# When the sums of x and of the attended values are made: moving three kinds of GpSimd sums, and the block moves of one batch, between slots of a fused attention kernel

## The chip, the cores and the metric

The kernel runs on one NeuronCore of one Trainium2 chip. The metric is the device time of one execution in microseconds. The program's instructions go to TensorE (PE; its weight loads are listed apart as PEld), VectorE (DVE), ScalarE (ACT), GpSimd (POOL) and SyncE (SP). In this kernel SP only issues DMAs, one after the other, in program order. Each engine takes its own instructions in program order too; they wait for each other through semaphores.

## What is computed

A cross-attention block in float32, with 8 batches of 256 rows and 1024 columns, 32 heads of width 32, and 256 keys per batch:

```python
mu  = x.mean(-1);  var = x.var(-1)
xn  = (x - mu) * rsqrt(var + 1e-5) * gamma + beta
Q   = split_heads(xn @ Wq.T)                 # 32 heads of 32
K = V = split_heads(ctx)                     # ctx: 8 x 256 x 1024
p   = softmax(where(mask, Q K^T / sqrt(32), -inf))
out = x + merge_heads(p V) @ Wout.T
```

## The kernel before

**Slots.** A batch has 8 groups of 4 heads (`NQ = 8`), so there are `N = 64` groups, and the main loop runs over them: slot n is one pass of `for n in range(N)`. The b-th batch's own slots are 8b to 8b+7; "first slot" is 8b, "seventh slot" is 8b+6. In slot n the program issues, in this order: the scores of group n+1 on PE (`scores(n + 1)`, L479), some steps of the output product of the batch before (`project_steps(n, 0)`, L694), the attended values of group n-2 (`values(n - 2)`, L622), more output steps (`project_steps(n, 1)`), the queries of a later group (`make_q`, L340, or `query_product`, L440), the softmax of group n+1, then the side work of the slot, with `project_steps(n, 2)` in its middle.

**Softmax of one group.** For each of 4 heads and 2 row blocks, DVE adds the mask and takes the minimum (L515), ACT takes the exponential with its row sum (L519); per head, DVE takes the reciprocal (`rden`, L526), POOL multiplies by it twice (L528; the function is `normalize`), and DVE transposes 32x32 blocks into `pT` (L534; `blocks`). ACT copies half of `pT` aside into `pc` (L540), and SP moves quarters between partitions (L600 `pT<-pT`, L604 `pT<-pc`). PE uses `pT` of the group three slots later, in its `values`. There are 4 buffers of `e`, 4 PSUM banks of scores, 3 of `pT`.

**Two products made with 7 multiplications instead of 8.** For batches 3 to 7 (`SPLIT = 3`) the query product is Winograd's form of a 2x2 block product, one multiplication in each of 7 slots from `first = 8 (b - 1) + 2` on (`firsts`; `Q_PRODUCTS`). It needs four sums of quarters of the normalized x, all on POOL (`sum_x`, L430): S1 = A21 + A22 and S2 = S1 - A11 into the two halves of `sums_x`, S4 = A12 - S2 and S3 = A22 - S2. S1 is used in slot `first`, S2 in `first + 3`. The output product of batches 0 to 6 has the same form (`PRODUCTS`), with four sums of quarters of the attended values (`sum_at`, L675): S3 = A11 - A21 (written over A21), S2 = A22 - S3, S4 = A12 - S2, S1 = S2 + A11. The first half of a batch's attended values is complete in its slot 8b+5, the second half in slot 8b+9. For S3 only the first half is needed.

**The first steps of an output product.** For batches 0 to 5, in slot 8(b+1)+1 PE makes four steps of A11 (8 PE instructions), ACT copies that partial result out of PSUM (`keep_p1`, L702, placed in the softmax after the exponentials of three heads), and only then three steps of A12 go on in the same PSUM bank. This is the slot in which PE makes no queries (except slot 17, which makes one).

**x on its way in.** For a batch b from 2 on, x is loaded, its statistics are taken (`ln_stats`, L226 and L231 on DVE, a power on POOL, L234, behind the sums of the slot), ACT normalizes it, DVE transposes blocks (`blocks_x`), and 16 DMAs of 64 KB put the blocks in place (`move_x`, L327, tile names `xnT<-xe`). The moves of a slot are issued on SP behind the DMAs of that slot's softmax. Batches 3 to 7 have their moves in slots first-6, first-5 and first-4 (4, 6 and 6). Batch 2's moves are in slots 5 to 8, four in each; its queries are first made in slot 10.

**Weights.** POOL also folds gamma into Wq (`fold`, L361), makes four sums of quarters of Wout (`sum_wo`, L183) and four of Wq (`sum_wq`, L391), by hand-written lists of slots. `keep_wq` (L397, L400) sends finished sums to DRAM, `load_ring` (L407) brings them back.

The lists are consulted at the end of a slot, in this order: moves, `keep_wq`, the mask's bias, `project_steps(n, 2)`, `sum_at`, `sum_x`, `add_p1`, the power of the statistics, and the sums of weights.

## Time and profile before

| | |
|---|---|
| time before, median of 3 runs | 592.53 us (591.06 to 595.61) |
| profiled execution, its own time | 590.59 us |
| its span | 588.8 us |
| granted TensorE clock, mean over the span | 0.994 |
| PE busy | 572.1 us, 97% |
| DVE / ACT / POOL busy | 453.9 / 412.1 / 396.7 us |
| DMA queue q1 | 117.74 MB, 67.8% of 16 engines' span |
| POOL idle ahead of S1 of x (L430), 4 times | 22.6 us |

The span is the time from the program's first to its last instruction in the profiled execution; the 1.8 us between 588.8 and 590.59 lie around it. A row of the groups gives the engine, the line, output and inputs, how often, then busy time and mean duration, and after the bar the idle time of the engine just ahead of it with what ended it. A busy PE is not PE at its peak: the ends of matmuls are modelled, and a matmul under a halved clock counts as busy for longer.

A slot can be found in the trace by the 16 matmuls of L479 with which it begins; the times of slots in this document are the starts of those groups.

### The profile page before, as it was taken

The numbers are of one execution on the slowest core, as the hardware profiler recorded it, in microseconds if no ns is written. First come the engines' busy times: TensorE is split into PE (matmuls) and PEld (weight loads), VectorE is DVE, ScalarE is ACT, GpSimd is POOL, SyncE is SP. The second block draws the span as 40 slices with busy tenths as digits, with TensorE's granted clock in tenths as the row PEclk, the third lists the DMA queues.
The fourth block names the chain that finished last, engine by engine and source line by source line (L and its number), as shares of the span: only waits on it lengthen the run. The fifth ranks groups of instructions, "written<-read, shape, count | busy, mean of one in ns | idle before, by whom it ended". The sixth has DMA issues, their size and how long they took to land.

```text
span 588.8 us, 20015 instructions
## 1 busy us (share of the span) xinstructions
PE 572.1 (97%) x7176; PEld 395.1 (67%) x7176; DVE 453.9 (77%) x1686; ACT 412.1 (70%) x1424; POOL 396.7 (67%) x663
## 2 busy tenths in 40 slices
PE   8999998999999999899999999799998999999997
PEld 8778884676676776577766776467774777754544
DVE  6898898787778887888888888678876778779801
ACT  4688877776578775796777877578775766769810
POOL 1787999789788985766576762857628466458720
PEclk9999999999999999999999999999998999999999
DMA  8675798755886777876878666776657764547661
GB/s 291 240 217 174 218 259 230 248 154 171 248 247 175 236 207 220 226 221 175 241 210 245 190 186 187 241 211 201 169 140 224 221 203 141 143 121 224 177 184 71
DMA packets 48051, 119.02 MB, mean 202 GB/s; under 512 B 9168, under 2 KB 9936, under 8 KB 47952
## 3 DMA queue, kind: packets, MB, share of 16 engines
q1 hardware_dynamic: 47664, 117.74, 67.8%
q8 instruction: 57, 0.93, 0.8%
q14 instruction: 42, 0.34, 0.2%
q10 hardware_dynamic: 288, 0.01, 0.0%
HBM read 66.33 MB, written 11.53 MB: 132 GB/s over the span
## 4 chain that ended last, share of the span: by engine, by line
PE 71%; DVE 7%; DMA 6%; POOL 6%; issue 4%; ACT 3%; SPq 2%; POOLq 0%; DVEq 0%; ACTq 0%
PE po_S L694 16%; PE pq L340 9%; PE pq_A L440 9%; PE sc L479 9%; PE pv L622 8%; PE po_A L694 7%; PE pq_S L440 6%; POOL e L528 4%; DMA pT<-pT 3%; PE po L744 3%; DVE pT L534 3%; ACT e L519 2%; DVE e L515 2%; DMA x<-in_x_dram 1%; PE po_last L744 1%
## 5 line engine op out<-in xcount | busy, mean ns | idle before, releaser
L528 POOL TENSOR_SCALAR e<-e,rden 128x256 f32<-128x256 f32 x512 | 236.4, 482 | 124.5 <-DVE rden L526 123.1
L519 ACT ACTIVATE e<-e,mn 128x256 f32<-128x256 f32 x512 | 254.0, 501 | 54.6 <-DVE mn L515 54.6
L534 DVE STREAM_TRANSPOSE pT<-e 128x512 f32<-128x512 f32 x256 | 180.8, 706 | 60.1 <-POOL e L528 51.1
L515 DVE CUSTOM_DVE_ANT_0 e<-sc,mb 128x256 f32<-128x256 f32 x512 | 186.0, 416 | 32.6 <-PE sc L479 32.3
L540 ACT COPY pc<-pT 128x512 f32<-128x512 f32 x128 | 79.0, 617 | 78.9 <-DVE pT L534 39.8
L519 ACT ACTIVATION_READ_ACCUMULATOR e<-e,mn 128x1 f32 x512 | 97.8, 191 | 0.0
L340 PE MATMUL pq<-xnT,wq 128*128 128x256 f32 (+1 forms) x368 | 84.2, 383 | 2.4 <-DMA xnT<-xe 2.4
L340 PEld LDWEIGHTS pq<-xnT,wq 128*128 128x128 f32 x368 | 68.6, 190 | 17.1 <-issue 3.8
L479 PEld LDWEIGHTS sc<-k,qa 32*128 32x128 f32 x1024 | 46.4, 185 | 43.6 <-issue 25.5
L622 PE MATMUL pv<-pT,v 64*32 64x128 f32 x4096 | 74.5, 274 | 0.0
L694 PE MATMUL po_S<-wo,at 128*128 128x512 f32 x152 | 74.3, 606 | 0.0
L622 PEld LDWEIGHTS pv<-pT,v 64*32 64x32 f32 x4096 | 57.2, 105 | 25.3 <-issue 11.9
L479 PE MATMUL sc<-k,qa 32*128 32x256 f32 x1024 | 74.0, 402 | 0.1
L694 PE MATMUL po_A<-wo,at 128*128 128x512 f32 x128 | 63.9, 635 | 9.6 <-ACT p L702 8.1
L694 PE MATMUL po_S<-wo,s 128*128 128x512 f32 x104 | 50.1, 605 | 0.0
L694 PEld LDWEIGHTS po_A<-wo,at 128*128 128x128 f32 x128 | 23.2, 195 | 36.0 <-issue 22.8
L515 DVE DVE_READ_ACCUMULATOR2_ANT mn<- 128x1 f32 x512 | 42.6, 83 | 0.0
L526 DVE RECIPROCAL rden<-den 128x2 f32<-128x2 f32 x256 | 37.7, 147 | 5.7 <-ACT e L519 4.5
L440 PEld LDWEIGHTS pq_A<-xnT,wq 128*128 128x128 f32 x320 | 37.3, 192 | 4.8 <-issue 4.1
L694 PEld LDWEIGHTS po_S<-wo,at 128*128 128x128 f32 x152 | 25.8, 190 | 19.8 <-issue 19.1
L440 PE MATMUL pq_A<-xnT,wq 128*128 128x128 f32 x320 | 37.3, 275 | 0.0
L635 ACT COPY at<-pv 128x128 f32<-128x128 f32 x128 | 26.2, 254 | 10.3 <-PE pv L622 10.3
(89 smaller groups left out, 595.3 us busy)
## 6 DMA issues: line engine op xcount, KB each, us to landing
v<-in_kv_dram SPq DMA_DIRECT2D x32, 512.0 KB, 5.2
pT<-pT SPq DMA_DIRECT2D x128, 128.0 KB, 3.3
pT<-pc SPq DMA_DIRECT2D x128, 128.0 KB, 4.4
ring<-kept_T SPq DMA_DIRECT2D x18, 512.0 KB
k<-in_kv_dram SPq DMA_DIRECT2D x32, 256.0 KB, 3.9
x<-in_x_dram SPq DMA_DIRECT2D x14, 512.0 KB
r<-in_x_dram SPq DMA_DIRECT2D x28, 256.0 KB, 5.1
out_dram<-r SPq DMA_DIRECT2D x28, 256.0 KB, 3.0
```

Source lines behind the costliest of these rows:

```text
L340: nc.tensor.matmul(pqs[n], wq[:, o, c, :], xnTs[b](c), start=(c == 0), stop=(c == NC - 1),)
L440: nc.tensor.matmul(pqs[b][:, o, :], w[:, c], x_[:, c], start=begins and o + c == 0, stop=c == NK - 1, skip_group_check=True,)
L479: nc.tensor.matmul(scs[n][j][:, s, :], qa[r, n % NQ, ts(s, P)], ks[n - n % 2][r, n % 2, :], start=True, stop=True,)
L515: nc.vector.tensor_tensor_reduce(out=e[:, s, :], in0=pss[j][:, s, :], in1=mbs[n // NQ], scale=1.0, scalar=NO_SCORE, op0=ALU.add, op1=ALU.m ...
L519: nc.scalar.activation(e[:, s, :], e[:, s, :], AF.Exp, bias=mn[:, s : s + 1], scale=-1.0, accum_out=den[:, s : s + 1],)
L526: nc.vector.reciprocal(rden, dens[j])
L528: nc.gpsimd.tensor_scalar(es[j][:, s, :], es[j][:, s, :], rden[:, s : s + 1], 1.0, ALU.mult, ALU.mult,)
L534: nc.vector.transpose(pT[:, :, :, j, :, :].rearrange("p a i s k -> p (a i) s k"), es[j].rearrange("p s (b t) -> p b s t", t=K),)
L540: nc.scalar.copy(pc[:, :, ts(j, 2)], pT[:, 1, :, ts(j, 2)])
L622: nc.tensor.matmul(pvs[n][r][j * HD : (j + 1) * HD], vs[n - n % 2][ts(r, 2 * K), i, ds(n % 2 * P + j * HD, HD)], pT[ts(r, 2 * K), :, i, j, ...
L635: nc.scalar.copy(ats[b, k][:, c, :, ts(r, 2), :], pv.rearrange("p a s k -> p s a k"))
L694: nc.tensor.matmul(po, operand(b, name)[:, c], wo[:, which, c], start=begins and c == 0, stop=c == NK - 1, skip_group_check=not begins,)
```

## The change

Four edits, all of them in when something is issued; no instruction is added or taken away.

1. **Sums of x.** S1 and S2 of batch b are both made in slot first-2 = 8(b-1), S1 ahead of S2. Before, S1 stood in first-3 for batches 4 to 7 and in first-2 for batch 3, S2 in first-2 for batches 4 to 7 and in first-1 for batch 3. S4 (first-1) and S3 (first+1) stay.
2. **S3 of the attended values.** Batch 0 keeps slot 8. Batch 1 has it in slot 15 instead of 16, batches 2 to 6 in their own seventh slot 8b+6 instead of 8b+8.
3. **Batch 2's moves of x.** Slots 5, 6 and 7 with 4, 6 and 6 moves, instead of four slots with 4 each.
4. **Sums of Wq.** T3's second block goes from slot 15 to 16, its third from 16 to 17; the DMA that keeps its first half goes from slot 16 to 17.

```diff
         elif b == 2:
             when = dict(
                 loads=(0, 1), stats=(2, 3), norms=(3, 3), trans=(4, 5),
-                moves=tuple(5 + i // 4 for i in range(16)),
+                moves=tuple(5 + (i + 2) // 6 for i in range(16)),
             )
...
-        (9, "T1", 0), (14, "T1", 1, 2), (15, "T1", 3), (15, "T3", 0, 1), (16, "T3", 2),
-        (18, "T3", 3), (19, "T2", 0), (20, "T2", 1, 2, 3), (21, "T4", 0, 1), (22, "T4", 2, 3),
+        (9, "T1", 0), (14, "T1", 1, 2), (15, "T1", 3), (15, "T3", 0), (16, "T3", 1),
+        (17, "T3", 2), (18, "T3", 3), (19, "T2", 0), (20, "T2", 1, 2, 3), (21, "T4", 0, 1), (22, "T4", 2, 3),
     ):
         sums[n] += [partial(sum_wq, which, o) for o in chunks]

+    S3_SLOTS = [(b, NQ * b + {0: NQ, 1: NQ - 1}.get(b, NQ - 2)) for b in range(B - 1)]
...
-        (9, "B11", 0), (10, "B11", 1), (15, "T1", 0), (16, "T1", 1), (16, "T3", 0), (19, "T3", 1),
+        (9, "B11", 0), (10, "B11", 1), (15, "T1", 0), (16, "T1", 1), (17, "T3", 0), (19, "T3", 1),
     ):
         away[n].append(partial(keep_wq, name, half))
...
         project_steps(n, 2)
+        for one, slot in S3_SLOTS:
+            if n == slot:
+                sum_at(one, "S3")
         if b >= 0:
-            for name in {0: ("S3",), 2: ("S4",), 3 if b == B - 2 else 5: ("S1",)}.get(i, ()):
+            for name in {2: ("S4",), 3 if b == B - 2 else 5: ("S1",)}.get(i, ()):
                 sum_at(b, name)
             if i == 0 and b == B - 2:
                 sum_at(b, "S2", slice(0, NK - 1))
-        for slot, name in ((n + 3, "S1"), (n + 2, "S2"), (n + 1, "S4"), (n - 1, "S3")):
-            if slot in firsts and firsts[slot] > SPLIT:
+        for slot, name in ((n + 2, "S1"), (n + 2, "S2"), (n + 1, "S4"), (n - 1, "S3")):
+            if slot in firsts:
                 sum_x(firsts[slot], name)
-        for slot, name in ((n + 2, "S1"), (n + 1, "S2"), (n + 1, "S4"), (n - 1, "S3")):
-            if firsts.get(slot) == SPLIT:
-                sum_x(SPLIT, name)
```

## The prediction

> **What bounds the kernel now.** I read the page first, then the waits, then the slots. The page's busy times and its chain:

> ```profile
> PE 572.1 (97%) x7176; PEld 395.1 (67%) x7176; DVE 453.9 (77%) x1686; ACT 412.1 (70%) x1424; POOL 396.7 (67%) x663
> PE 71%; DVE 7%; DMA 6%; POOL 6%; issue 4%; ACT 3%; SPq 2%; POOLq 0%; DVEq 0%; ACTq 0%
> ```

> PE is the bound: 97% busy, 71% of the chain. An edit that moves only POOL and SP work pays only where PE stands still. The waits show what POOL and PE lose:

> ```profile
> POOL sx L430 <- DMA xnT<-xe: 18.4, 3, 6.7
> POOL sx L430 <- DMA out_dram<-r: 4.2, 1, 4.2
> PE po_A L694 <- ACT p L702: 8.1, 4, 2.3
> PE pq L340 <- DMA xnT<-xe: 2.4, 1, 2.4
> ```

> POOL waits 22.6 us in four places ahead of S1 of x, for block moves that have not landed (the fourth is put down to `out_dram`, which SP issues right behind the moves). PE waits 8.1 us for the copy of P1, and 2.4 us once for moves. The timeline of slots 47 to 49 ties the first to the third:

> ```profile
> 434.47 3.75 SPq L327 DMA_DIRECT2D xnT<-xe  x6
> 441.39 1.26 POOL L430 TENSOR_TENSOR sx<-xnT 128x512 f32<-128x512 f32 x1 [6.16 <-DMA xnT<-xe]
> 442.64 1.84 POOL L528 TENSOR_SCALAR e<-e,rden 128x256 f32<-128x256 f32 x4
> 445.61 0.62 ACT L540 COPY pc<-pT 128x512 f32<-128x512 f32 x1 [3.56 <-DVE rden L526]
> 451.45 0.56 ACT L702 COPY p<-po_A 128x512 f32<-128x512 f32 x1
> 452.06 4.54 PE L694 MATMUL po_A<-wo,at 128*128 128x512 f32 x6 [2.33 <-ACT p L702]
> ```

> S1 (slot 47) sits 6.16 us in front of the normalizes of slot 48, so these start at 442.64. ACT's `pc` copy, behind them, comes 3.56 us late, the exponentials of slot 49 after it, then the copy of P1, and PE waits for that. The windows of slots 9, 10, 25, 33, 41 and 49 give the price (length, then PE busy, PEld, DVE, ACT, POOL, granted clock):

> ```profile
> 88.30:97.09 8.79, 8.70 (x95) 4.10 (x95) 6.74 (x29) 7.33 (x24) 8.59 (x14) 1.00 0.92 259
> 97.09:108.13 11.04, 8.63 (x104) 5.63 (x103) 8.73 (x31) 7.03 (x23) 9.87 (x16) 1.00 0.75 232
> 230.16:241.29 11.13, 8.70 (x95) 4.10 (x94) 9.50 (x32) 6.49 (x22) 9.38 (x17) 1.00 0.68 189
> 300.85:310.61 9.76, 8.63 (x95) 4.10 (x94) 8.13 (x29) 6.49 (x22) 8.59 (x15) 1.00 0.70 208
> 370.27:383.75 13.48, 10.00 (x96) 4.38 (x95) 10.90 (x34) 7.11 (x23) 11.74 (x21) 0.90 0.73 229
> 443.64:456.53 12.89, 10.40 (x96) 4.54 (x95) 9.71 (x32) 7.11 (x23) 11.15 (x18) 0.87 0.72 227
> ```

> Slots 9, 25, 33, 41 and 49 hold the same PE work. Slot 9 has no S1 ahead of it and takes 8.79; the others take 9.76 to 13.48, longer the longer POOL waited (4.2, 5.6, 6.2, 6.7 us give 9.76, 11.13, 12.89, 13.48).

> **S1 and S2 of x in slot first-2.** S1 now comes one slot later. Does it still wait? POOL was released, so the moves had landed, at 227.34, 296.65, 368.50 and 441.39 at the latest. In an undisturbed slot the normalizes end 7.75 us after its scores start (slot 39: scores 354.05, last normalize 361.80). Slots 24, 32, 40 and 48 start at 222.51, 293.20, 362.56 and 435.99, so S1 would be reached at 230.3, 301.0, 370.3 and 443.7: after the landing by 2.9, 4.3, 1.8 and 2.3 us. No wait. The cover of 1.8 to 4.3 us is what a later landing could use up before PE pays.

> POOL then makes S1 and S2 in a row: 1.27 + 1.28 = 2.55 us, to 232.8 in slot 24. The first reciprocal of slot 25 comes 3.5 us after its scores (354.05 to 357.54 in slot 39), at 233.7: 0.9 us later. Before, that slot held S3 of the attended values and S2 of x, as many. What is late next is the power of the statistics in slots 23, 31 and 39, until now behind S1: its input is ready at 224.1 (DVE 223.95 + 0.15), the normalizes it stands before start at 226.0. Nothing.

> With the wait gone, ACT starts the exponentials of slot 25 some 1.7 us (slot 48: 435.99 to 437.68) to 2.44 us (slot 9: 88.30 to 90.74) after the scores; 3.5 us later (448.49 to 452.01) the copy of P1 ends, at 5.2 to 5.96 us. PE reaches A12 at 1.08 + 3.63 + 1.09 = 5.8. So PE waits 0 to 0.16, as in slot 9. I take 8.79 for each: 2.34 + 0.97 + 4.69 + 4.10 = 12.1, and 0.34 from slot 42, whose start still ran at half clock (8.85 against 8.51 in its like): **12.4 us**. The ends: 13.1 with no wait at all (8.63), 11.3 if the four still wait some 0.4 us.

> [...] The gaps here are 2.3 us, yet the clock falls to 0.90 and 0.87 in just the two slots with the longest stalls, and their PE busy time rises from 8.70 to 10.00 and 10.40. [...] By the rows they belong to the stalls (in slot 41 a second one of 1.16 us precedes) and go: 12.4. All slots with short stalls show 1.00; I take the rows.

> **S3 of the attended values, two slots earlier.** Its input is complete one slot before, so no wait. It adds 1.28 us to POOL in slots 22, 30, 38, 46 and 54. In slot 46 and its likes POOL idles 2.7 us on the reciprocal: hidden. Slot 22 is full: T4's last two sums stand behind S3 and end at 217.4 instead of 216.1, the third at 216.1. PE's A22 product of slot 23 starts at 217.13 and comes to that third block 1.8 us later, at 218.9: 2.8 us of cover, so 0; 1.28 us if it is gone. In slot 15 S3 falls into 2.42 us in which POOL waits for the statistics (150.3 to 152.7): free.

> [...]

> **Batch 2's moves in three slots.** Before, the last four go out in slot 8, at 98.26 to 101.3, and PE's queries of slot 10 start at 102.79 instead of about 100.2. Now slot 7's six go out from 90.80 to about 94.6; with the median 3.2 us to landing they are there at 98: 2 us of cover. Slot 10 falls from 11.04 to its PE busy 8.63: **2.4 us**. On SP slots 6 and 7 carry two issues more, 2 x 0.62 = 1.2 us, and slot 8 four fewer (3.05 us). Behind slot 7's moves stands `pT<-pT` at 93.98; the values that it feeds start at 109.2. Hidden. What is late next is POOL, which idles only 0.3 us a slot up to there: in slot 11 its work before ends at 109.1, and its first normalize, 111.70, would now be due at 109.3. Just enough; if POOL cannot follow, the gain is 0 to 1.7.

> **T3 and its DMA.** One POOL sum passes from slot 15 to 16 and one from 16 to 17, as S3 comes into slot 15 and S2 of x into 16: 3 sums of 512 columns in each of the three slots, as before. The DMA (0.41 us of SP) goes from 167.43 to about 173.7; T2's first sum, which overwrites what it reads, starts at 189.89. Nothing.

> **Sum.** 12.4 + 2.4 = 14.8 us. Against the profiled execution's own 590.59 (span 588.8 and 1.8 around it) that is 575.8; this execution is 1.9 us under the median of 592.53, which gives 577.7 for a median. I say 577.5.

> **Rivals.** *ACT stays the bound of slot first-1.* The copy of P1 comes behind six exponentials in any case. If every such slot stops at the mildest now seen, 9.76, the gain is 1.4 + 3.7 + 3.1 + 0.3 + 2.4 = 10.9: 581.6. For it: slots 33 and 9 differ by only 1 us. Against it: in slot 33 ACT's `pc` copy is late by a POOL wait too (1.79 us). *The waits of POOL are not PE's.* Then only slot 10 gains: 590.1. Against it: the order of the four lengths follows the four waits. *The wait moves along with S1 (slower).* SP issues the moves behind `pT` copies that POOL's normalizes pace. If with these earlier the last move came as late against S1 as now, POOL would wait 22.6 us one slot nearer to the P1 copy, with 0.9 us of slack each instead of about 3: 19 us on PE instead of 9.1, and four half-clock stretches instead of two, +3.4, less the 2.4 of slot 10: 592.5 + 10.9 = 603.4. It decides from landings over 2.7 to 5.2 us later (1.8 to 4.3 plus 0.9). Against it: these moves belong to slot first-4, and nothing ahead of them changes.

> **Chances.** Forecast 0.72, ACT bound 0.18, only slot 10 0.06, slower 0.04. A measurement of this kernel can tell about 1% from no change, 5.9 us; the first two pass it. So faster 0.90, same 0.06, slower 0.04. The range goes from 573.0 (13.1 + 2.4 off 590.59, and some 2 us for the run) to 584.0 (past the first rival, with half of slot 10's gain lost).

> **What would show it.** In the changed profile the row `sx<-xnT` has no idle time ahead of it and slots 25, 33, 41 and 49 take 8.6 to 9.0 us at a clock of 1.00; PE's wait for P1 falls from 8.1 to under 1; `pq L340 <- DMA xnT<-xe` is gone and slot 10 takes about 8.6. Wrong if a wait ahead of `sx<-xnT` of over 2 us stays, if slots 25 to 49 stay over 9.7 without it, or if slots 11 to 16 grow by what slot 10 loses.

## The result, and the profile after

The changed kernel takes 578.68 us (median of 4 runs, 577.78 to 578.80), the kernel before beside it 593.16 us (591.06 to 595.61): 0.9751 of the time, 95% interval 0.9711 to 0.9791, which is 14.5 us with an interval of some 12.4 to 17.1. In a second set of runs the same changed kernel came to 0.9729 (0.9701 to 0.9756) of the kernel before. Runs over 1.5% above the fastest of their set are left out of all ratios and means here. The profiled execution took 578.70 us, its span 576.9 us; that is 11.9 us under the profiled execution of before, which was one of its faster runs.

The page of the changed kernel: busy time of the engines, then the chain by engine.

```profile
PE 568.4 (99%) x7176; PEld 393.6 (68%) x7176; DVE 454.1 (79%) x1686; ACT 411.7 (71%) x1424; POOL 397.6 (69%) x663
PE 80%; POOL 7%; DVE 4%; DMA 4%; issue 2%; ACT 1%; SPq 1%; DVEq 0%; POOLq 0%; ACTq 0%
```

The instructions are the same in number. PE went from 97% to 99% busy, from 71% to 80% of the chain, and its busy time itself fell by 3.7 us: nearly all of that is time at half clock which is gone (1.4, 1.8 and 0.3 us in slots 41, 49 and 42). The longest waits of POOL, then those of PE (engine, line, what ended the wait, us in total, times, longest):

```profile
POOL e L528 <- DVE rden L526: 125.8, 92, 4.7
POOL rstd L234 <- DVE ve L231: 24.0, 8, 6.9
POOL r L720 <- ACT ends L712: 0.7, 1, 0.7
```

```profile
PE pq L285 <- DMA wq<-in_wq_dram: 1.4, 1, 1.4
PE busy L120 <- POOL ring masks.py:199: 1.3, 1, 1.3
PE po_A L694 <- issue: 0.8, 1, 0.8
PE po_S L694 <- DVE r L736: 0.7, 2, 0.4
PE po_A L694 <- DMA wo<-in_woT_dram: 0.6, 1, 0.6
PE po_A L694 <- ACT qa L349: 0.4, 1, 0.4
```

No row of `sx` is left: 22.6 us of POOL's waiting ahead of S1 are gone. PE's 8.1 us for the copy of P1 and its 2.4 us for the moves are gone too. POOL now waits longer for the statistics (24.0 against 17.2 us), ahead of which S1 used to stand, and nobody waits for that. What is new are short waits of PE for Wout and for `qa` (for `r` it waited before too, 1.3 us), and 1.4 us for a load of Wq ahead of slot 0. The windows of slots 9, 10, 25, 33, 41 and 49 (length, then busy time of PE, PEld, DVE, ACT and POOL, granted clock, DMA share, GB/s):

```profile
89.11:99.21 10.10, 8.97 (x96) 4.02 (x95) 7.85 (x31) 7.33 (x24) 9.79 (x16) 1.00 0.92 254
99.21:108.19 8.98, 8.62 (x103) 5.62 (x102) 5.37 (x25) 4.33 (x16) 4.75 (x7) 1.00 0.80 250
231.02:239.58 8.56, 8.56 (x95) 4.10 (x94) 6.47 (x26) 5.97 (x21) 6.51 (x11) 1.00 0.90 272
299.85:308.42 8.57, 8.57 (x96) 4.11 (x95) 6.49 (x26) 5.97 (x21) 6.54 (x12) 1.00 0.82 263
367.98:376.55 8.57, 8.57 (x96) 4.11 (x95) 6.49 (x26) 5.97 (x21) 6.54 (x12) 1.00 0.94 320
436.10:444.66 8.56, 8.56 (x95) 4.10 (x94) 6.31 (x25) 5.97 (x21) 6.17 (x11) 1.00 1.02 329
```

Slots 25, 33, 41 and 49 take 8.56 to 8.57 us, all of it PE busy, at a clock of 1.00. Slot 10 lost 2.05 us, but slot 9 took on 1.31.

Between the two profiled executions the time by slot moved so: slots 25, 33, 41 and 49 by -2.57, -1.20, -4.91 and -4.33, slot 42 by -0.34, slot 10 by -2.05, slot 9 by +1.31, slots 11, 15 and 26 by +0.28, +0.50 and +0.72; the stretch ahead of slot 0 was 0.78 longer. All other slots are within 0.07 us of before.

### The profile page after: what moved, and what is told of

Read it like the earlier page. It is cut to its first block, busy times and chain, and to the rows that moved or that the text cites. A ratio compares the mean times of both kernels' runs of the same rounds, so it can differ in the third digit from the quotient of the medians.

```text
span 576.9 us, 20009 instructions
## 1 busy us (share of the span) xinstructions
PE 568.4 (99%) x7176; PEld 393.6 (68%) x7176; DVE 454.1 (79%) x1686; ACT 411.7 (71%) x1424; POOL 397.6 (69%) x663
## 4 chain that ended last, share of the span: by engine, by line
PE 80%; POOL 7%; DVE 4%; DMA 4%; issue 2%; ACT 1%; SPq 1%; DVEq 0%; POOLq 0%; ACTq 0%
PE po_S L694 18%; PE pq_A L440 16%; PE pv L622 10%; PE sc L479 10%; PE po_A L694 10%; PE pq_S L440 6%; PE pq L340 6%; POOL e L528 5%; PE po L744 3%; DVE e L515 2%; DMA wo<-in_woT_dram 2%; PE po_last L744 1%; DMA wq<-in_wq_dram 1%; ACT e L519 1%; DVE pT L534 1%
## 5 line engine op out<-in xcount | busy, mean ns | idle before, releaser
L528 POOL TENSOR_SCALAR e<-e,rden 128x256 f32<-128x256 f32 x512 | 237.0, 483 | 127.3 <-DVE rden L526 125.8
L540 ACT COPY pc<-pT 128x512 f32<-128x512 f32 x128 | 79.0, 617 | 71.7 <-DVE pT L534 43.0
L340 PE MATMUL pq<-xnT,wq 128*128 128x256 f32 (+1 forms) x368 | 84.1, 383 | 0.0
L340 PEld LDWEIGHTS pq<-xnT,wq 128*128 128x128 f32 x368 | 68.7, 190 | 14.3 <-issue 3.9
L694 PE MATMUL po_S<-wo,at 128*128 128x512 f32 x152 | 74.5, 607 | 0.3 <-DVE r L736 0.3
L694 PE MATMUL po_A<-wo,at 128*128 128x512 f32 x128 | 61.0, 609 | 1.9 <-issue 0.8
L694 PE MATMUL po_S<-wo,s 128*128 128x512 f32 x104 | 50.2, 606 | 0.4 <-DVE r L736 0.4
L526 DVE RECIPROCAL rden<-den 128x2 f32<-128x2 f32 x256 | 37.5, 147 | 6.2 <-ACT e L519 4.9
L694 PEld LDWEIGHTS po_A<-wo,at 128*128 128x128 f32 x128 | 22.5, 189 | 26.9 <-issue 21.7
L694 PEld LDWEIGHTS po_S<-wo,at 128*128 128x128 f32 x152 | 25.6, 190 | 20.8 <-issue 19.3
```

The costliest lines, as they stand in the source:

```text
L340: nc.tensor.matmul(pqs[n], wq[:, o, c, :], xnTs[b](c), start=(c == 0), stop=(c == NC - 1),)
L526: nc.vector.reciprocal(rden, dens[j])
L528: nc.gpsimd.tensor_scalar(es[j][:, s, :], es[j][:, s, :], rden[:, s : s + 1], 1.0, ALU.mult, ALU.mult,)
L540: nc.scalar.copy(pc[:, :, ts(j, 2)], pT[:, 1, :, ts(j, 2)])
L694: nc.tensor.matmul(po, operand(b, name)[:, c], wo[:, which, c], start=begins and c == 0, stop=c == NK - 1, skip_group_check=not begins,)
```

## The experiments

Two theories to begin with. **W**: the wait ahead of S1 is the loss of slots 25 to 49, by the path S1, normalizes, ACT, copy of P1, PE. Its rival **R**: what counts is how much work POOL has in a row, and the room that S3 leaves. For slot 10, the prediction's 2.4 us stood against **Q**, formed from the profile after: the earlier moves hand the time on through SP's queue to slots 9, 11 and 15.

### One edit at a time

**The sums of x alone.**

```diff
-        for slot, name in ((n + 3, "S1"), (n + 2, "S2"), (n + 1, "S4"), (n - 1, "S3")):
-            if slot in firsts and firsts[slot] > SPLIT:
+        for slot, name in ((n + 2, "S1"), (n + 2, "S2"), (n + 1, "S4"), (n - 1, "S3")):
+            if slot in firsts:
                 sum_x(firsts[slot], name)
-        ...
```

> The kernel before with the edit of the sums of x alone (S1 and S2 in slot first-2); S3 of the attended values, batch 2's moves and T3 stay as before. Theory W (POOL's wait for landed moves ahead of S1, which passes through the normalizes and ACT to the copy of P1, is the whole gain): some 12 us below before, about 581, with no idle time ahead of the row sx<-xnT and slots 25, 33, 41 and 49 at 8.6 to 9.2 us. Rival R (the room that the moved S3 leaves on POOL is needed): slot first-2 now carries three sums, 3.8 us, 0.4 us past the first reciprocal of slot first-1, so slots 25 to 49 stay at 9.5 or more and at least a third of the gain is missing, 585 or more.

579.33 us, 0.9791 (0.9749 to 0.9833): 12.4 us of 592, with an interval of 9.9 to 14.9. Slots 25, 33, 41 and 49 take 8.56 to 8.57. POOL's busy time there is about one sum higher than in the changed kernel (7.80 and 7.73 in slots 25 and 33, against 6.51 and 6.54):

```profile
230.87:239.44 8.57, 8.57 (x96) 4.11 (x95) 6.54 (x26) 5.97 (x21) 7.80 (x13) 1.00 0.93 318
299.56:308.12 8.56, 8.56 (x95) 4.10 (x94) 6.48 (x26) 5.97 (x21) 7.73 (x13) 1.00 0.72 197
```

R falls: a third sum in slot first-2 costs nothing. This edit alone is nearly the whole of the change.

**S3 of the attended values alone** (the list `S3_SLOTS` and its loop, put into the kernel before).

> The kernel before with S3 of the attended values in its new slots alone. Theory W: the wait ahead of S1 stays (about 22 us of POOL in four places), so within 1 us of before; POOL's sums in slots 24, 32, 40 and 48 are one fewer, which may take up to 1.3 us off each of slots 25, 33, 41 and 49, if those are late by POOL's work and not only by its wait: then up to 5 us below before. Rival R (room on POOL is what counts): 6 us or more below before.

592.54 us, 0.998 (0.9943 to 1.0017): no difference. POOL still waited 22.3 us ahead of S1, and slots 25 to 49 took 9.63 to 12.71.

**Batch 2's moves alone.**

```diff
-                moves=tuple(5 + i // 4 for i in range(16)),
+                moves=tuple(5 + (i + 2) // 6 for i in range(16)),
```

> The kernel before with the edit of batch 2's moves alone (4, 6 and 6 in slots 5 to 7). The prediction's step: slot 10 falls from 11.04 to 8.6 and nothing else grows, 2.4 us below before. Theory Q (SP's queue hands it on: the two further moves of slot 6 hold back the loads of x and of Wout behind them, those of slot 7 the load of the residual, and POOL, which has no time to spare up to slot 16, sets the pace there): slot 10 falls by about 2 us, slots 9, 11 and 15 grow by as much together, start of slot 0 to start of slot 16 within 0.5 us of before, time within 1 us of before.

588.20 us, 0.9947 (0.9910 to 0.9984): 3.1 us, with an interval of 0.9 to 5.3. In its profiled execution slot 10 fell to 9.50, but slots 9 and 15 grew to 10.07 and 8.94, and PE waited for Wout and for `r`, as the changed kernel's did (here in slots 9 and 10):

```profile
97.63 1.13 PE L694 MATMUL po_A<-wo,at 128*128 128x512 f32 x2 [0.98 <-DMA wo<-in_woT_dram]
106.31 1.96 PE L694 MATMUL po_S<-wo,s 128*128 128x512 f32 x4 [0.88 <-DVE r L736]
```

In this execution slot 0 to slot 16 took 129.4 us, against 128.8 in the kernel before: no gain there, as Q says. That its time still lay 4.6 us below the profiled execution of before came from slots 25, 33, 41 and 49: 41.8 us together against 47.3, with the wait ahead of S1 still in place. These stalls differ from one execution to the next (44.1 with S3 alone), so the timed 3.1 us cannot be put down to the length of slot 10.

**The changed kernel without that edit.**

> The changed kernel with batch 2's moves back in slots 5 to 8. The prediction's step: 2.4 us above the changed kernel, 581. Theory Q: within 0.7 us of the changed kernel (578.0 to 579.4), slot 10 back at 11.0, slots 9, 11 and 15 back at 8.8, 9.25 and 8.45.

579.22 us, 0.9804 (0.9751 to 0.9857). Slots 9, 10, 11 and 15 were back at 8.84, 11.07, 9.25 and 8.39. Against 0.9751 and 0.9729 of the changed kernel it is 3 to 4.5 us more, with intervals that overlap: it favours the prediction's 2.4 without proving it. The single runs say where it comes from. The changed kernel's ten, over both sets, lay between 575.7 and 578.8 us, all at a mean granted clock of 0.999 or 1.00. Of the six here, three at a clock of 1.00 took 576.9 to 578.5, as long as the changed kernel; the other three, at 0.997, took 580.0 to 583.2. So in these few runs the old moves cost nothing where the clock held; the loss came with the lower clock. One stretch of 3.41 us at half clock is 0.003 of the mean, and the only pause of PE over 2 us in the profiled execution is the one of slot 10 (2.37 us).

### Is it the wait, or S1's place?

**S1 stays in slot first-3, the moves land one slot earlier.** In the kernel before:

```diff
-                moves=tuple(first - 6 + (i + 2) // 6 for i in range(16)),
+                moves=tuple(first - 6 + i // 8 for i in range(16)),
```

> The kernel before, S1 left in slot first-3, but the moves of batches 3 to 7 in two slots of eight (first-6 and first-5) instead of three, so that they land one slot ahead of S1. Theory W (the wait for the moves is the loss, wherever S1 stands): no or little idle time ahead of sx<-xnT, slots 25, 33, 41 and 49 at 8.6 to 9.0, clock 1.00, some 12 us below before, about 581. Rival (POOL's order of work is the loss: S1 behind slot first-3 holds back the normalizes also without a wait, by its own 1.27 us): half of the gain or less, 587 or more.

580.33 us, 0.9833 (0.9779 to 0.9888). The waits of POOL in this kernel:

```profile
POOL rstd L234 <- DVE ve L231: 19.9, 8, 7.2
POOL sx L430 <- DMA xnT<-xe: 1.3, 2, 0.7
```

1.3 us ahead of S1 where there were 22.6, and slots 25 to 49 at 8.56 to 8.57. W is shown from the other side: with S1 where it was and only the landing made earlier, the stalls are gone. The time came out 2.5 us higher than with the sums moved, within both intervals; in this execution slot 10, with its moves as before, took 12.4 us, and its pause of 2.10 us was followed by half clock. The one timed run at a clock of 1.00 took 577.2 us, the other five, at 0.997 or less, 579.7 to 583.5.

**S1 and S2 one more slot later**, in first-1, from the changed kernel:

```diff
-        for slot, name in ((n + 2, "S1"), (n + 2, "S2"), (n + 1, "S4"), (n - 1, "S3")):
+        for slot, name in ((n + 1, "S1"), (n + 1, "S2"), (n + 1, "S4"), (n - 1, "S3")):
```

> The changed kernel with S1 and S2 of x yet one slot later, in first-1 with S4 behind them: three sums of x and S2 of the attended values there, 5.1 us of POOL, and S1 ends some 2 us into slot first, where PE's first query product wants it about 2.2 us in. Theory W (only a wait ahead of the P1 copy costs): slots 25 to 49 stay at 8.6, slots 26, 34, 42 and 50 grow by 0 to 1.5 us each, 0 to 6 us above the changed kernel. Rival (POOL's amount of work in a row decides, not the wait): the normalizes of slot first+1 come late, the copies behind them too, more than 8 us above.

577.78 us, 0.9787 (0.9743 to 0.9831) of a kernel before that came to 592.02 here: within the scatter of the changed kernel. Slots 25 to 49 stayed at 8.56. S1 of batch 7 ended at 446.77 (445.48 + 1.29), PE's first query product began at 447.28: half a microsecond later. A slot later still was not tried; it would come after that use.

### The clock

**PE kept at work through the stall.** The kernel before, with matmuls that compute nothing of use in slots 41 and 49:

```diff
         project_steps(n, 1)
+        if n in (41, 49):
+            fill_pe = ps_q.tile([P, 512], F32, tag="pq", name=f"fill_{n}")
+            for _ in range(16):
+                nc.tensor.matmul(
+                    fill_pe[:, :P], wo[:, B11, 0, :P], wo[:, B11, 0, :P], start=True, stop=True,
+                )
```

> The kernel before, with 16 matmuls of 128x128 into an unused PSUM bank put on PE in slots 41 and 49, ahead of the three steps that wait for the copy of P1; they compute nothing that is used and fill some 1.8 of the 2.3 us that PE stands still. By the rows (the stall itself lowers the clock): the granted clock stays at 1.00 in slots 41 and 49, the six matmuls behind the copy take 2.6 us instead of 4.1 to 4.5, the two slots end near 12 instead of 13.5 and 12.9, 2.5 to 3.5 us below before. [...]

593.32 us, 1.0049 (1.0014 to 1.0084): half a per cent longer. The filler was sized wrongly: 16 matmuls are 32 instructions on PE and took 3.7 us (381.58 to 385.26), not 1.8, and so outlasted the copy of P1 (ended at 383.92 in slot 41). The windows of slots 10, 25, 33, 41 and 49:

```profile
96.97:109.62 12.65, 10.32 (x104) 6.77 (x103) 8.71 (x31) 7.21 (x23) 10.81 (x16) 0.87 0.76 249
231.52:243.59 12.07, 8.70 (x95) 4.10 (x94) 9.60 (x32) 6.49 (x22) 10.33 (x19) 1.00 0.70 206
303.14:315.49 12.35, 10.34 (x95) 4.70 (x95) 10.65 (x36) 7.11 (x23) 10.60 (x17) 0.86 0.68 203
375.13:387.93 12.80, 12.21 (x128) 7.68 (x127) 10.77 (x34) 7.11 (x23) 11.05 (x19) 1.00 0.75 223
447.48:459.62 12.14, 12.14 (x128) 7.68 (x127) 8.82 (x31) 7.11 (x23) 10.44 (x16) 1.00 0.67 204
```

The two filled slots kept a clock of 1.00, which proves little by itself: with S3 alone the unfilled slots 41 and 49 had pauses of 2.33 us and kept it too. Slots 10 and 33, not filled, fell to 0.87 and 0.86, after pauses of 2.33 and 2.01 us. The timed comparison says nothing on the clock's price, since the filler cost more than it could save, but the profile shows pauses of 2 us after which the clock halves.

### Where slots 9 to 15 get it back

The changed kernel again, as the measure of the three that follow it:

> The changed kernel again, on the same chip as the three that follow, as their measure: 578.7 within 0.7 us. Slot 9 again at 10.1 and slot 10 at 9.0, with PE waiting in slot 9 for the last load of Wout, if that is the program's and not one execution's.

577.35 us, 0.9729 (0.9701 to 0.9756). From the start of slot 0 to that of slot 16 it took 127.0 us, in the first profiled execution of the same program 128.9 (before: 128.8). Slot 9 took 9.61, and PE waited for `qa` in it instead of for Wout: what holds slot 9 differs from one execution to the next. The same program came out 1.3 us lower than in the first set (578.68), so smaller differences than that say little.

**Moves 6, 4, 6:**

```diff
-                moves=tuple(5 + (i + 2) // 6 for i in range(16)),
+                moves=tuple(5 if i < 6 else 6 if i < 10 else 7 for i in range(16)),
```

> The changed kernel with batch 2's moves 6, 4 and 6 in slots 5 to 7 instead of 4, 6 and 6. Theory Q (the two further moves of slot 6 hold back the loads of x and Wout issued behind them): with slot 6 back at four moves PE no longer waits in slot 9 for the load of Wout, slot 9 falls from 10.1 towards 8.8, some 1 us below the changed kernel, less what the two moves now cost in slot 5. Rival (it is the six moves of slot 7, or the traffic as a whole): slot 9 stays at about 10.1 and the time equals the changed kernel's within 0.5 us.

577.85 us, 0.9736 (0.9708 to 0.9764), slot 9 at 9.54: the same. **Moves 8, 4, 4** (`5 if i < 8 else 6 if i < 12 else 7`):

> The changed kernel with batch 2's moves 8, 4 and 4 in slots 5 to 7. Theory Q: slots 6 and 7 issue as in the kernel before, so slot 9 is 8.8, slot 10 8.4 to 8.6 (its moves have landed), slot 11 9.25: 1.5 to 2.5 us below the changed kernel, if four further issues in slot 5 (2.5 us of SP) are hidden. Rival (POOL, with no time to spare up to slot 16, sets the pace there): slot 0 to slot 16 stays at 128.9 us whatever SP does, and the time within 0.5 us of the changed kernel.

577.59 us, 0.9728 (0.9698 to 0.9758): the same. Slot 10 fell to 8.39 and slot 11 stood at 9.25, but slot 9 took 10.39, with PE held by Wout although SP issued no more moves in slots 6 and 7 than before:

```profile
PE po_A L694 <- DMA wo<-in_woT_dram: 1.2, 1, 1.2
```

This does not speak against SP's queue as the cause. The eight moves of slot 5 had already set SP back, as the issues of the x load of slot 6 and of the last load of Wout show:

```profile
82.20 0.43 SPq L130 DMA_DIRECT2D x<-in_x_dram  x1
87.36 0.45 SPq L173 DMA_DIRECT2D wo<-in_woT_dram  x1
```

From the start of slot 0 that is 59.5 and 64.7 us, where the kernel before has 57.5 and 63.6. Only the number of issues in slots 6 and 7 is ruled out as what decides.

**Loads of Wout ahead of those of x** in slots 0 to 7, of which 6 and 7 matter here (the block with `load_wo` put ahead of `between += [partial(load_x, ...)]`):

> The changed kernel with the loads of Wout of slots 0 to 7 issued ahead of the loads of x of the same slot, so in slots 6 and 7 the last two loads of Wout go out one 512 KB load earlier. Theory Q: PE's wait of 0.6 us for Wout in slot 9 goes, slot 9 falls from 10.1 to about 9.3, up to 0.8 us below the changed kernel; the loads of x, now later, may cost DVE some tenths at the statistics. Rival (POOL sets the pace): no change over 0.5 us.

580.49 us, 0.9779 (0.9752 to 0.9805): 3 us slower. Waits of PE and of DVE in slots 8 and 9:

```profile
PE po_A L694 <- ACT qa L349: 3.4, 1, 3.4
DVE st L226 <- DMA x<-in_x_dram: 3.1, 1, 3.1
```

Now x lands late; the statistics stand in the middle of DVE's work for the softmax, and PE gets the 3.1 us as 3.4. Slot 9 took 13.69, with a stretch at half clock behind that pause (0.88 over the slot).

**The second half of batch 3's x one slot later** (loads in slots 6 and 8, statistics in 8 and 10, from the changed kernel):

```diff
-                loads=(first - 12, first - 11) if b == SPLIT else (first - 13, first - 12),
-                stats=(first - 10, first - 9) if b == SPLIT else (first - 11, first - 9),
+                loads=(first - 12, first - 10) if b == SPLIT else (first - 13, first - 12),
+                stats=(first - 10, first - 8) if b == SPLIT else (first - 11, first - 9),
```

> The changed kernel with the second load of batch 3's x in slot 8 instead of 7 and its statistics in slot 10 instead of 9, so that the last load of Wout stands behind one 512 KB load fewer. Theory Q in its last form (what PE waits for in slot 9 is Wout's landing, which the traffic of slots 6 and 7 sets): slot 9 falls from 9.6 to 10.1 towards 8.8, slot 10 stays at 8.4 to 9.0, up to 1.2 us below the changed kernel, 576.5. Rival (POOL sets the pace up to slot 16): no change over 0.5 us.

577.84 us, 0.9779 (0.9732 to 0.9825). Slot 9 did fall to 8.76. What held it came with that x load, then: Wout's landing behind it, or the statistics of slot 9 that wait for it; the edit moves both, so this run does not tell them apart. But slot 11 rose to 10.22 (DVE waited 3.6 us for the residual `r`). No gain. What PE waits for in slots 9 to 11 (Wout, `qa`, `r`) changes from one of these four kernels to the next. None of them beats the changed kernel.

## Why the prediction was right, and where it was not

**Sum.** 577.5 predicted, 578.68 measured; 14.8 us of gain predicted, 14.5 measured. That it came so close is in part luck. Between the profiled executions the gain was 11.9, not 14.8: the four slots gave 0.9 more than was taken, but slot 10 gave 2.05 instead of 2.4, slots 9, 11 and 15 took 2.1 back, slot 26 0.7, and the stretch ahead of slot 0 was 0.8 longer. What made up for it is the 1.9 us that was added because the profiled execution of before lay under its median; the one of the changed kernel lay at its median (578.70 and 578.68).

**The wait ahead of S1.** As predicted in place, path and size: no idle time ahead of `sx<-xnT`, slots 25 to 49 at 8.6, clock 1.00; 12.4 us predicted for it, 12.4 measured with that edit alone (9.9 to 14.9, so the equal digits are chance). The path is shown by the two experiments that take the wait away in different ways.

**The copy of P1.** Taken: 8.79 for each of the four slots, by slot 9's 0.16 us of waiting. Measured: 8.56 to 8.57; the copy of P1 in slot 49 ends 5.5 us after the scores (441.03 + 0.57 - 436.10), ahead of PE's arrival at 5.8. The four slots of the profiled pair gave 13.0 us where 12.1 was taken. Slot 26 took 0.72 back, at a wait for nothing that the profile shows (the slot is 0.3 to 1.7 us longer in six of the fourteen profiled executions, and not in the others, the second one of this same program among them); its cause is open.

**POOL's slack of 0.9 us in slot first-1.** The step asked for no more than it needed, and the cover is much larger than it said: three sums instead of two in slot first-2, or all of them one slot later, cost nothing measurable. The normalizes may start some time after their reciprocal before PE notices.

**S3 and T3.** Taken at 0; S3 measured 0.998 (0.9943 to 1.0017). T3 was not tried alone. In their new slots the 20 sums of L430 take 1264 to 1283 ns, beside VectorE's work as before; in the kernel before they took 1258 to 1297 ns.

**Batch 2's moves: the step that was only half right.** Slot 10 fell as predicted. But "Hidden" was said of SP's further issues with only `pT<-pT` in view. Behind slot 6's moves stand the loads of x and of Wout, behind slot 7's that of the residual. SP's issues of the x load of slot 6 and of the first residual, in the kernel before and in the changed one:

```profile
79.66 0.46 SPq L130 DMA_DIRECT2D x<-in_x_dram  x1
95.81 0.44 SPq L150 DMA_DIRECT2D r<-in_x_dram  x1
```

```profile
82.42 0.44 SPq L130 DMA_DIRECT2D x<-in_x_dram  x1
100.57 0.44 SPq L150 DMA_DIRECT2D r<-in_x_dram  x1
```

With the 0.78 us of the longer start taken off they went out 2.0 and 4.0 us later. Slot 7's six moves, taken to go out from 90.80 to 94.6, went out from 93.92 to 98.63. DVE then waited 3.2 us for a residual, and PE 0.6 us for Wout in slot 9 and 0.4 us for `r` in slot 10. In the first pair of profiles all 2.1 us came back in slots 9, 11 and 15, and 1.3 of them in slot 9, which the prediction's own sign of being wrong (slots 11 to 16) left out; in the second execution of the changed kernel 1.9 us stayed.

All profiled executions with one of the two sets of moves, and the loads as they were, tell the same. From slot 0 to slot 16 the old moves took 128.8 to 129.4 us in the three in which slot 10 kept its clock, and 130.4 to 131.3 in the three in which it fell to half; the new ones 127.0 to 129.4 in four, none at half clock. So the 2.4 us of the pause come back in large part in the neighbours, and what the edit takes away for good is the chance of a half-clock stretch behind that pause. The prediction had no such term for slot 10. That the timed runs (3.1 us for the edit alone, 0.9 to 5.3) hold its 2.4 is luck.

**The clock.** The 3.0 us by which PE's busy time was higher in slots 41 and 49, and the 0.34 us of slot 42, were put down to the stalls, and that held: both half-clock stretches went with the stalls (clock 1.00 in slots 41 and 49 of the changed kernel), and in the kernel with the filler half clock followed pauses of 2.01 and 2.33 us (0.86 over slot 33, 0.87 over slot 10). But the rows were read too simply. The clock did not fall in slots 41 and 49 because their stalls were the longest: PE's pauses in slots 10 and 25, 2.41 and 2.33 us, were as long as theirs (2.32 and 2.33), and those slots show 1.00. What differs in the traces is how the pauses lay in time (last section), so that this execution had two such stretches was in all likelihood luck.

**The rivals.** That ACT would stay the bound (581.6) and that only slot 10 would gain (590.1) are out: the four slots went to 8.6. The wait did not move along with S1. Even a slot later there was none, since the moves had long landed. The 9.1 us that this rival's 19 are set against are the 12.4 less the 3.0 and 0.34 us of half clock.

## What to carry to other kernels

Find the engine with slack whose wait is passed on, and follow it step by step to the bound engine: here 22.6 us of GpSimd waiting cost TensorE some 12, because the wait stood ahead of the normalizes in GpSimd's order of work (S1 of slot 47 waited 6.16 us, and the normalizes of slot 48 behind it started at 442.64, as S1 ended). Then it is enough to make the waiting instruction one slot later or what it waits for one slot earlier; both gave nearly the same. When transfers are brought forward, list every transfer that stands behind them in the same queue and when it is needed: where the transfers stand close, a gain in one slot can come back in its neighbours (here 2.05 us gained in slot 10, and 2.1 us back in slots 9, 11 and 15). And where TensorE pauses for some 2 us, count the half-clock stretch that may follow beside the pause itself: the two in the kernel before made up some 3.5 us of PE's busy time, and in slot 10 such a stretch outweighed what was left of the pause.

## What the runs showed of the hardware that was not expected

The trace of the kernel before shows where its two lie. The granted clock rose at 5.61 us (the matmuls of L120, 128x128 each, start 0.21 us apart up to there and 0.11 us apart from there on). The stretches begin at 381.08 and 452.76 and last 3.413 us each; counted from the rise, they begin after 110 and 131 times 3.413 us. Cut into steps of that length from the rise on, the trace shows a difference between the pauses: how much of a pause falls into one step. The steps around the pauses of slots 10 and 41 in the kernel before (length, PE busy, granted clock, DMA share, GB/s; what PE busy leaves of 3.41 is the pause):

```profile
97.77:101.18 3.41, 2.61 (x78) 1.00 0.71 198
101.18:104.59 3.41, 1.80 (x8) 1.00 0.50 115
377.67:381.08 3.41, 1.40 (x4) 1.00 0.88 258
381.08:384.49 3.41, 3.41 (x12) 0.50 0.60 190
```

The pause of slot 10, 2.41 us, is cut in two, 0.80 and 1.61, and the clock holds. Of the one of slot 41, 2.32 us, 2.01 lie in one step, and the next step runs at half clock. So it is with the 2.33 us of slot 49, all in the step from 449.35 on. With the sums of x alone, even slot 10's pause of 2.97 us leaves the clock as it is, cut into 1.43 and 1.54:

```profile
98.69:102.10 3.41, 1.98 (x66) 1.00 0.56 177
102.10:105.51 3.41, 1.87 (x9) 1.00 0.72 150
105.51:108.92 3.41, 3.41 (x13) 1.00 1.00 329
```

Of all steps of the kernel before between its first and last slot, those two, with 2.33 and 2.01 us of pause, have the most; the next have 1.61 and 1.52 us, with a clock of 1.00 behind them. In the changed kernel none has more than 0.76 us, and none is followed by half clock. There the clock rose at 5.82 us instead of 5.61, so the steps lay differently against the program; that it is chance whether a pause of 2 us is cut in two is the author's estimate from this, and no run tried it.

It shows in the times too. Of the kernel before, 7 runs at a mean clock of 0.997 took 587.9 us on average, 13 at 0.994 took 591.2, 15 at 0.991 took 592.5 and 7 at 0.988 took 594.1; each 0.003 is one more stretch. So these stretches go with a good part of its spread (585.8 to 596.2 us, against 575.7 to 578.8 without these stalls); runs of equal clock still differ by up to 7.6 us, and why was not tried.
